# Attention and FFN layer in 32-bit floats: the norm's scaling one tile ahead of its transposition, and the splits of one FFN operand two chunks earlier

## The chip, the cores and the metric

The kernel runs on one core of a Trainium2 chip. The core has a matrix engine (TensorE, PE in the profile), a vector engine (VectorE, DVE), an activation engine (ScalarE, ACT), a general engine (GpSimd, POOL) and a queue engine (SyncE, SP). Each works through its own instructions in order, and they wait for one another by semaphores. Transfers are issued here from SyncE and from POOL. The metric is the device time of one execution in microseconds (us). The profile gives one execution in detail.

## The reference

The input is x, 2 sequences of 2048 tokens, each token a row of 1024 floats. There are two residual sublayers, with a plain layer norm LN ahead of each:

```
y   = x + Attn(LN(x))
out = y + FFN(LN(y))

Attn(z): q, k, v = z Wqkv + bqkv          (256 columns each, one head)
         softmax(q k^T / 16) v Wo + bo
FFN(z):  shared = relu(z up)^2 down        (1024 -> 2048 -> 1024)
         routed = ((z fc1) expert) * r fc2  (latent 512; r: sum of the two largest gate logits)
         LN(shared + routed) * gamma + beta
```

Everything is float32.

## The kernel before

**Precision.** A product of float32 matrices is made of three passes: each operand is split into a high part (rounded by a cast on ScalarE, `xh`, `xha`) and a low part (the rest, by a subtraction on VectorE, `xl`, `xla`), and TensorE sums high x high, low x high and high x low (`Pass3.add`, the matmul is line 130). `split` (lines 142 and 143) issues both parts at once. `split_late` (149 and 150) issues the cast and keeps the subtraction back until the next `flush()`.

**Tiles.** The 4096 tokens are 8 blocks of 512, and each block is 4 tiles of 128 tokens (`NB` = 4). A normalised tile must reach TensorE with the features on the partitions. For that, `transpose_write` transposes 32 x 32 pieces on VectorE (line 213), and a transfer writes the result to a scratch tensor in HBM (`xt_d`, line 218). `fetch_tile` reads it back in another layout (`xt`, line 224), and a split makes the operand of it.

**The q/k/v stage.** Blocks are taken in the order 4 to 7, then 0 to 3; the text counts them in that order from 0 (i = 0 to 7). `qkv_block` makes four tiles of v, then two chunks each of q and k. Its matmuls per block are 96 of 256 columns for v and 96 of 512 columns for q and k. After each piece j it calls `after(j)`, which places work for the next block: after the v tiles, `NormBlock.step(0)` to `step(3)` and then `step(4)` norm, transpose, write and fetch the next block's tiles. After pieces 5, 6 and 7 the first three of them are split. The fourth is split after the first v tile of the next block (`x3`). ScalarE's evictions of q (439) and k (442) stand between these splits.

`NormBlock` has two kinds of statistics. `Moments` makes them on ScalarE (259 to 272, tiles 0 and 2), `Stats` on VectorE (178 to 182, 292, tiles 1 and 3). `normalise` is then the same for both: a reciprocal (276) and a product (282) on VectorE, and the scaling of the row on ScalarE (283).

**What sets the order.** The first seven blocks of this stage, and the whole FFN, stand under `tc.manual_schedule()`: each engine's instructions come in the order in which the code issues them. The last q/k/v block and the attention are ordered by the library's planner. Row buffers are a pool of nine, and large operands are a pool of fourteen. Loads by SyncE for the attention's start (`q_d`, `Wo`) wait for such rows. From i = 4 on, `sum_step` adds 2 MB copies of weights to POOL's queue at the end of a block.

**The FFN.** It takes two blocks (1024 tokens) per pass, b = 0 to 3. Both of its matrix products are made with seven quarter products, named p1 to p7, whose operands are sums and differences of quarters. The loop over `UP` makes the first product in chunks of 12 matmuls: m = 0 to 19 are the interleaved chunks of p1 and p2, m = 20 to 29 are p4, then p6, p5, p3 and p7. The operand of p4 is the split of the second block's tiles (`x_t[1]`, half 1). `X["p4"]` takes its two buffers from the pool, and one tile is split after each of four odd chunks. Each chunk begins with `flush()`. Its result is evicted from the accumulator by ScalarE or VectorE (lines 1000 and 1091 for p2 and p1, 1094 for the latent chunks of p2). Up to chunk 15 the loop also carries the output of the pass before (`out_step`). In pass 0 the second block's norm runs inside these same chunks (`norm2.step`). In later passes it is done in the pass before.

Of the kernel before, what the change touches and what calls it, by code (L numbers as in the profile page):

```python
# [25 lines left out]
def kernel(  # L26
# [33 lines left out]
    NB = W // P  # L60
# [20 lines left out]
    def unit(name, dtype=FR):  # L81
        return up.tile([P, U], dtype, tag="u", name=name)
# [7 lines left out]
    def half(name):  # L90
        return hp.tile([P, W], FP, tag="h", name=name)
# [48 lines left out]
    def split(t, hi, lo, eng=nc.vector):  # L140

        nc.scalar.copy(hi, t)  # L142
        eng.tensor_tensor(lo, t, f32(hi), ALU.subtract)
# [8 lines left out]
    def flush():  # L152
        for f in late_ops:
            f()
        late_ops.clear()
# [55 lines left out]
    def transpose_write(r, q=nc.gpsimd):  # L211
        b = row("xblk")
        nc.vector.transpose(  # L213
            b.rearrange("p (q k i) -> p q k i", q=P // SQ, i=SQ),
            r.rearrange("p (k i q) -> p q k i", k=NCC, i=SQ),
        )
        d = dram.tile([P, C], FP, tag="xt", name="xt_d", bufs=8)
        q.dma_start(out=d, in_=b)
        return d

    def fetch_tile(d, q=nc.gpsimd):

        xt = row("xt")
        q.dma_start(
            out=xt.rearrange("p (a f) -> p a f", a=P // SQ),
            in_=d.rearrange("(a i) (q f) -> (i q) a f", i=SQ, q=P // SQ),
        )
        return xt
# [13 lines left out]
    def split_x(xts, half, t, X, split=split):  # L242
        xv = xts[t].rearrange("p (a k j) -> p k a j", k=NCC, j=SQ)[:, ts(half, NCC // 2)]
        hi, lo = (
            v.rearrange("p (c n) -> p c n", n=W)[:, :, ts(t, P)].rearrange(
                "p c (a j) -> p c a j", j=SQ
            )
            for v in X
        )
        split(xv, hi, lo)  # L250
# [46 lines left out]
    class NormBlock:  # L297
# [5 lines left out]
        def step(self, t):  # L303
            rows, m = self.rows, self.m
            if t == 0:
                m += [Moments(rows[0], "n"), Stats(rows[1])]
                m[0].second()
            if t < NB:
                m[t].normalise()
                if t == 0:  # L310
                    m.append(Moments(rows[2], "n"))
                    m[2].second()
                self.d.append(transpose_write(rows[t]))
                if t == 0:
                    m.append(Stats(rows[3]))
            if t:
                self.x.append(fetch_tile(self.d[t - 1]))
# [19 lines left out]
    def piece(pr, c, n, sl):  # L337
        return tuple(v.rearrange("p (c n) -> p c n", n=n)[:, c, sl] for v in pr)
# [13 lines left out]
    NK = (NIC + NLC) // 2  # L352
# [354 lines left out]
    for n in range(1, NBLK + 1):  # L707
        if n == NBLK:
            X = {p: (unit("xh"), unit("xl")) for p in ("p1", "p2")}
# [117 lines left out]
    def next_piece():  # L827

        while (pieces or staged or cast) and len(ready) < 3:
            if cast:  # L830
                end_piece()
            while pieces and len(staged) < 2:
                stage()
            if staged and not cast:
                cast_piece()
        return ready.pop(0)
# [3 lines left out]
    def acc_bank(name):  # L840
        n_bank[0] += 1
        return bank(psb if n_bank[0] % 3 == 2 else psa, name)
# [153 lines left out]
    def new_x():  # L996
        return unit("xh"), unit("xl")

    def relu(o, v):
        nc.scalar.activation(o, v, AF.Relu)  # L1000

    def square(v):
        nc.scalar.activation(v, v, AF.Square)

    t1 = xts
    with tc.manual_schedule():
        for b in range(NBB):
            if b == 0:
                norm2 = Norm(1)
            x_t = [t1, None]  # L1010
# [3 lines left out]
            def h_at(name, i, n=1):  # L1014

                if i < HU // P:
                    key, q = (name, i // 4), i % 4
                else:
                    key, q = (name in ("11", "12"), "l"), i - HU // P
                    q += 2 * (name in ("12", "21"))  # L1020
                if key not in h:
                    h[key] = unit(f"h{b}", FP)
                return h[key][:, ds((q + 1 - n) * W, n * W)]
# [54 lines left out]
            for m, (p, i) in enumerate(UP):  # L1078
                flush()
                w = next_piece()  # L1080
                if p != "p2":
                    acc[i] = Pass3(acc_bank("pu"), NCC // 2)
                ps = acc[i].ps
                if p == "p2":
                    acc[i].more()
                for c in range(NCC // 2):
                    acc[i].add(piece(w, c, P, slice(0, P)), piece(X[p], c, W, slice(0, W)))
                lat, pair = i >= HU // P, i % 2 and i < HU // P
                c22, c21 = h_at("22", i), h_at("21", i) if m >= 2 * NK else None
                if p == "p1":  # L1090
                    nc.scalar.copy(c22, ps)
                elif p == "p2":
                    if lat:
                        add(h_at("11", i), ps, rwb[0], ALU.mult)
                    else:
                        relu(h_at("11", i), ps)
                        if pair:
                            square(h_at("11", i, 2))
                elif p == "p4":
                    nc.scalar.copy(c21, ps)  # L1100
                elif p == "p6":
                    add(c22, ps, c22, ALU.subtract)
                    add(c21, c21, c22, ALU.subtract)
                elif p == "p5":
                    add(c22, c22, ps, ALU.add)
                elif p == "p3":
                    c12 = h_at("12", i)
                    add(c12, c22, ps, ALU.add)  # L1108
                    if lat:
                        add(c12, c12, rwb[0], ALU.mult)  # L1110
                    elif pair:
                        relu(h_at("12", i, 2), h_at("12", i, 2))
                        square(h_at("12", i, 2))
                else:
                    add(c21, c21, ps, ALU.add)
                    add(c22, c22, ps, ALU.subtract)
                    if lat:
                        add(c21, c21, rwb[1], ALU.mult)
                        add(c22, c22, rwb[1], ALU.mult)
                    elif pair:  # L1120
                        for v in ("21", "22"):
                            relu(h_at(v, i, 2), h_at(v, i, 2))
                            square(h_at(v, i, 2))

                if m % 2 and m < 15:
                    out_step()
                if b == 0 and m in (0, 1, 2, 4, 6, 8, 9, 10, 11, 12, 13):
                    norm2.step()

                if m == 12:  # L1130
                    x_t[1] = norm2.x
                    X["p4"] = new_x()
                if m >= 13 and m % 2 and m < 2 * NK:
                    split_x(x_t[1], 1, (m - 13) // 2, X["p4"], split_late)
                elif m >= 2 * NK and p != "p7":
                    n = {"p4": "p6", "p6": "p5", "p5": "p3", "p3": "p7"}[p]
                    if i == 1:
                        X[n] = new_x()
                    if i % 2 and i < 2 * NB:
                        if p == "p4":  # L1140
                            sums_x(x_t, i // 2)
                        r_, f_ = PLACE[n]
                        split_x(x_t[r_], f_, i // 2, X[n], split_late)

                if m == 0:
                    ga = half("ga")[: 2 * NE, :]
                    nc.scalar.copy(ga, gate_part(X["p1"], 0))
                elif m == 2:
                    gs = half("gs")[: 2 * NE, :]
                    add(gs, ga, gate_part(X["p2"], 1), ALU.add)  # L1150
                    gt = Gate(gs)
                elif (p, i) == ("p4", 1):
                    add(ga, ga, gate_part(X["p4"], 1), ALU.add)
                elif (p, i) == ("p7", 0):
                    add(ga, ga, gate_part(X["p7"], 0), ALU.subtract)
                    gt = Gate(ga)
                if m == 6 or (p, i) == ("p7", 3):
                    gt.largest()
                elif m == 10 or (p, i) == ("p7", 6):
                    rwb[p == "p7"] = gt.spread()  # L1160
                if p == "p7" and i >= NK - 5:
                    step_s()
            X = {}
# [15 lines left out]
            for j, p in enumerate(("p1", "p2", "p6", "p5", "p3", "p7", "p4")):  # L1179
# [12 lines left out]
                for k in range(NK - late):  # L1192
# [4 lines left out]
                    if more:  # L1197
# [3 lines left out]
                        if j >= 5 and k % 2 and k < 2 * NB:  # L1201
                            n = "p1" if j == 5 else "p2"
# [98 lines left out]
```

## Time and profile before

| | us |
|---|---|
| runs | 2402.42, 2394.48, 2394.49 |
| median of the runs | 2394.49 |
| profiled execution | 2396.25 |
| its span | 2394.2 |
| TensorE busy | 2341.5 (98%) |
| VectorE busy | 1461.7 (61%) |
| ScalarE busy | 1133.1 (47%) |
| POOL busy | 297.9 (12%) |
| q/k/v stage, about | 40 to 319 |
| attention, about | 319 to 790 |
| FFN, about | 790 to the end |

The span runs from the first to the last instruction; the execution's own time is 2.05 us longer. A row of a timeline has the start in us, the duration, the engine and line of code, the operation, what it writes and reads, and in brackets how long the engine had been idle before it and what ended that wait. A row of waits has the waiting engine and instruction, what it waited for, the total in us, how many times, and the longest. A row of a table by stretches has the stretch, its length, the busy time of each engine with the number of instructions, the granted share of TensorE's clock, the busy share of the DMA engines and the GB/s.

### The profile page before, as it was taken

Reading aid. Unit: us, or ns where it says so; the run is one execution under the profiler, and the core shown is the slowest. Engines: PE = TensorE matmul, PEld = TensorE weight load, DVE = VectorE, ACT = ScalarE, POOL = GpSimd, SP = SyncE. Lnnn points to the kernel's source line nnn. Section 1 sums busy time; section 2 is a strip of 40 time slices with the busy share of each in tenths; the row PEclk is TensorE's granted clock in tenths of the full one; section 3 lists DMA queues with packets and bytes.
Section 4 is the critical chain, followed back from the end, with each engine's and each line's share of the span. In section 5 each row is a group of like instructions: output and inputs, shape, how many; then the busy total and the mean of one; then the engine's idle time right before and its main releaser. Section 6 shows DMA issues by size and latency. Waiting matters only on the chain.

```text
span 2394.2 us, 29276 instructions
## 1 busy us (share of the span) xinstructions
PE 2341.5 (98%) x10704; PEld 1924.4 (80%) x10704; DVE 1461.7 (61%) x2168; ACT 1133.1 (47%) x1846; POOL 297.9 (12%) x450
## 2 busy tenths in 40 slices
PE   8999899999998999999999999999999999999998
PEld 7888778888886778788777888877888887788886
DVE  5566549888876466797736468644446662435545
ACT  5555445555544553676552274644146354214224
POOL 3322110111110010111210011210000010000001
PEclk9999999999999999999999999999999999999999
DMA  5877883999996666687997779997657799655695
GB/s 187 313 249 270 293 199 101 274 318 318 292 274 180 210 229 192 214 275 255 332 309 234 241 275 333 321 339 249 194 182 268 259 329 296 205 193 185 202 310 191
DMA packets 225807, 603.99 MB, mean 252 GB/s; under 512 B 18768, under 2 KB 80720, under 8 KB 223616
## 3 DMA queue, kind: packets, MB, share of 16 engines
q1 hardware_dynamic: 152160, 334.02, 41.1%
q0 software_dynamic: 73504, 268.11, 36.7%
q8 instruction: 85, 1.39, 0.2%
q14 instruction: 58, 0.48, 0.1%
HBM read 448.96 MB, written 210.76 MB: 276 GB/s over the span
## 4 chain that ended last, share of the span: by engine, by line
PE 78%; issue 9%; DMA 5%; DVE 3%; ACT 3%; POOL 2%; SPq 0%; POOLq 0%; DVEq 0%; ACTq 0%
PE pu L130 30%; PE pd L130 26%; PE ps L130 7%; PE po L130 7%; PE pw L130 3%; PE pg L870 1%; DMA w<-wt 1%; PE pf L130 1%; DMA xt<-xt_d 1%; PE pq L130 1%; DMA w<-w_p 1%; DMA w_p<-w 1%; DVE xblk L213 1%; PE psum L617 1%; ACT xrow L283 1%
## 5 line engine op out<-in xcount | busy, mean ns | idle before, releaser
L130 PE MATMUL pd<-w,sp 128*128 128x512 f32 x3336 | 763.9, 391 | 9.3 <-DVE sp L1055 6.2
L130 PEld LDWEIGHTS pd<-w,sp 128*128 128x128 f32 x3336 | 627.6, 188 | 144.4 <-DVE sp L1055 9.0
L130 PE MATMUL pu<-xh,w 128*128 128x512 f32 x2240 | 694.7, 391 | 7.4 <-ACT w L813 5.9
L130 PEld LDWEIGHTS pu<-xh,w 128*128 128x128 f32 x2240 | 419.6, 188 | 99.0 <-ACT w L813 6.9
L130 PE MATMUL pu<-xl,w 128*128 128x512 f32 x1120 | 436.6, 390 | 2.9 <-DVE xl L150 2.8
L130 PEld LDWEIGHTS pu<-xl,w 128*128 128x128 f32 x1120 | 210.4, 188 | 48.3 <-DVE xl L150 4.6
L1050 ACT CAST sp<-h 128x512 fp32r<-128x512 f32 x238 | 145.7, 618 | 187.9 <-PE pd L130 157.4
L1055 DVE TENSOR_TENSOR sp<-h,sp 128x512 fp32r<-128x512 f32 x238 | 162.4, 688 | 101.0 <-ACT sp L1050 100.7
L813 ACT CAST w<-w 128x512 fp32r<-128x512 f32 x210 | 128.2, 616 | 184.4 <-DMA w<-wt 158.8
L821 DVE TENSOR_TENSOR w<-w 128x512 fp32r<-128x512 f32 x210 | 143.3, 687 | 89.3 <-ACT w L813 84.6
L130 PE MATMUL po<-p,v 128*128 128x512 f32 x768 | 196.4, 393 | 1.4 <-ACT p L142 1.2
L130 PE MATMUL ps<-q,k 128*128 128x512 f32 x768 | 195.9, 393 | 1.9 <-DVE max L560 1.8
L130 PEld LDWEIGHTS ps<-q,k 128*128 128x128 f32 x768 | 142.3, 188 | 36.2 <-DVE max L560 6.9
L130 PEld LDWEIGHTS po<-p,v 128*128 128x128 f32 x768 | 143.5, 189 | 32.2 <-ACT p L142 2.0
L1000 ACT ACTIVATE h<-h 128x1024 f32<-128x1024 f32 x48 | 50.7, 1055 | 208.9 <-DVE h L1108 159.9
L824 POOL DMA_DIRECT2D w_p<-w x140 | 75.5, 539 | 584.3 <-DVE w L821 535.4
L555 ACT COPY s<-ps 128x512 f32<-128x512 f32 x128 | 74.9, 585 | 148.0 <-PE ps L130 147.4
L213 DVE STREAM_TRANSPOSE xblk<-xrow 128x1024 f32<-128x1024 f32 x60 | 120.6, 2010 | 39.0 <-ACT xrow L283 37.7
L150 DVE TENSOR_TENSOR xl<-xt,xh 128x512 fp32r<-128x512 f32 x104 | 71.6, 688 | 119.1 <-ACT xh L149 119.1
L560 DVE TENSOR_TENSOR max<-ps,max 128x512 f32<-128x512 f32 x120 | 82.5, 688 | 44.3 <-ACT s L555 43.9
L130 PE MATMUL pq<-xha,w_h 128*128 128x512 f32 x256 | 99.7, 389 | 0.0
L130 PE MATMUL pq<-xha,w_l 128*128 128x512 f32 x256 | 99.7, 389 | 0.0
(181 smaller groups left out, 3043.1 us busy)
## 6 DMA issues: line engine op xcount, KB each, us to landing
w<-w_p SPq DMA_DIRECT2D x350, 512.0 KB, 3.7
w_p<-w POOLq DMA_DIRECT2D x140, 512.0 KB, 4.6
w<-wt SPq DMA_DIRECT2D x210, 256.0 KB, 3.8
xt_d<-xblk POOLq DMA_DIRECT2D x56, 512.0 KB, 3.5
xt<-xt_d POOLq DMA_DIRECT2D x56, 512.0 KB, 6.4
wt<-in_L_ffn_up_w_dram POOLq DMA_DIRECT2D x9, 2048.0 KB, 26.1
wt<-in_L_ffn_down_w_dram POOLq DMA_DIRECT2D x9, 2048.0 KB, 33.8
xres<-in_L_attn_x_dram SPq DMA_DIRECT2D x32, 512.0 KB, 13.2
```

The costliest lines, as they stand in the source:

```text
L130: nc.tensor.matmul(self.ps, lhsT=a, rhs=b, start=self.i == 0, stop=self.i == self.n - 1, skip_group_check=self.on,)
L150: late_ops.append(lambda: nc.vector.tensor_tensor(lo, t, f32(hi), ALU.subtract))
L213: nc.vector.transpose(b.rearrange("p (q k i) -> p q k i", q=P // SQ, i=SQ), r.rearrange("p (k i q) -> p q k i", k=NCC, i=SQ),)
L283: nc.scalar.activation(self.v, self.v, AF.Identity, scale=rs, bias=nb)
L555: nc.scalar.copy(s["s"][k // 4][:, ts(k % 4, W)], pm)
L560: nc.vector.tensor_tensor(s["max"], pm, s["max"], ALU.max)
L813: nc.scalar.copy(w[:, 0:W], f32(w)[:, W : 2 * W])
L821: nc.vector.tensor_tensor(w[:, W : 2 * W], v[:, W : 2 * W], v[:, 0:W], ALU.subtract)
L824: nc.gpsimd.dma_start(out=kept[key], in_=w.bitcast(FP))
L1000: nc.scalar.activation(o, v, AF.Relu)
L1050: nc.scalar.copy(t[:, 0:W], v)
L1055: add(t[:, W : 2 * W], v, f32(t)[:, 0:W], ALU.subtract)
```

## The change

In `NormBlock.step` the scaling moves one tile ahead. At t = 0 the first tile is normalised, the statistics of tile 2 follow, then tile 1 is normalised, and only then is tile 0 transposed. At t = 1 and 2 the next tile is normalised ahead of the transposition of the present one. At t = 3 there is only the transposition.

In the FFN's first loop the operand of p4 takes its buffers at m = 10 instead of 12 in passes 1 to 3, and its four splits stand after chunks 11, 13, 15 and 17 instead of 13, 15, 17 and 19. Pass 0 keeps 12 and the old places.

```diff
@@ NormBlock.step
             if t == 0:
                 m += [Moments(rows[0], "n"), Stats(rows[1])]
                 m[0].second()
+                m[0].normalise()
+                m.append(Moments(rows[2], "n"))
+                m[2].second()
+
+            if t + 1 < NB:
+                m[t + 1].normalise()
             if t < NB:
-                m[t].normalise()
-                if t == 0:
-                    m.append(Moments(rows[2], "n"))
-                    m[2].second()
                 self.d.append(transpose_write(rows[t]))
                 if t == 0:
                     m.append(Stats(rows[3]))
@@ the FFN's loop over UP
-                if m == 12:
+                m4 = 12 if b == 0 else 10
+                if m == m4:
                     x_t[1] = norm2.x
                     X["p4"] = new_x()
-                if m >= 13 and m % 2 and m < 2 * NK:
-                    split_x(x_t[1], 1, (m - 13) // 2, X["p4"], split_late)
+                if m > m4 and (m - m4) % 2 and (m - m4) // 2 < NB:
+                    split_x(x_t[1], 1, (m - m4) // 2, X["p4"], split_late)
                 elif m >= 2 * NK and p != "p7":
```

## The prediction

> **What bounds the kernel now.** I read the page first, for the engine that sets the end.
>
> ```profile
> span 2394.2 us, 29276 instructions
> ...
> PE 2341.5 (98%) x10704; PEld 1924.4 (80%) x10704; DVE 1461.7 (61%) x2168; ACT 1133.1 (47%) x1846; POOL 297.9 (12%) x450
> ...
> PE 78%; issue 9%; DMA 5%; DVE 3%; ACT 3%; POOL 2%; SPq 0%; POOLq 0%; DVEq 0%; ACTq 0%
> ```
>
> TensorE is busy 98% of the span and carries 78% of the chain that ended last. The built program of the changed kernel has the same TensorE instructions in the same order, so the change can only win or lose time in which TensorE stands still or runs slowly. Next, TensorE's own waits: all of the span's 53 us of idle time is in few places, and three kinds lie where the diff works.
>
> ```profile
> PE pu L130 <- ACT w L813: 5.9, 1, 5.9
> PE pv L130 <- ACT xha L142: 5.9, 1, 5.9
> PE pu L130 <- DVE xl L150: 2.8, 3, 0.9
> PE pv L130 <- DVE xla L143: 1.8, 5, 0.4
> ```
>
> The first row (start of the FFN) is outside the change. The second and fourth are q/k/v blocks that wait for a split tile of the next block; the third is the first chunk of p4 in the FFN passes b = 1, 2, 3. Then the timelines of the seventh block (i = 6), where the long wait arises, one engine after another:
>
> ```profile
> 265.02 1.99 DVE L213 STREAM_TRANSPOSE xblk<-xrow 128x1024 f32<-128x1024 f32 x1 [1.31 <-ACT xrow L283]
> ...
> 269.23 2.03 DVE L213 STREAM_TRANSPOSE xblk<-xrow 128x1024 f32<-128x1024 f32 x1 [1.31 <-ACT xrow L283]
> ...
> 271.55 0.53 POOL L218 DMA_DIRECT2D xt_d<-xblk  x1 [2.93 <-DVE xblk L213]
> ...
> 279.07 0.77 POOL L224 DMA_DIRECT2D xt<-xt_d  x1 [6.22 <-issue]
> ...
> 271.28 0.88 SPq L192 DMA_DIRECT2D xrow<-q_d  x2
> ...
> 285.90 1.14 ACT L142 CAST xha<-xt 128x512 fp32r<-128x512 f32 x2 [12.15 <-DMA xt<-xt_d]
> ...
> 288.19 0.58 PE L130 MATMUL pv<-w_h,xha 128*128 128x256 f32 x1 [5.87 <-ACT xha L142]
> ```
>
> The fourth tile is transposed at 269.23, written at 271.55, fetched back at 279.07 and cast at 285.90. In ScalarE's queue that cast stands ahead of the casts of the third tile, for which TensorE waits from 282.3 to 288.2.
>
> **The change, part 1: the norm.** Nothing is added or removed: per block the same four sets of a reciprocal (0.16), a product (0.16) on VectorE and a scaling (1.24) on ScalarE are issued one tile earlier. No DMA is in the moved step. Now each tile costs VectorE 4.21 us from one transposition to the next (260.82, 265.02, 269.23): 1.99 of transposition, about 0.3 + 0.3 for a v tile's bias and low half, 0.35 for reciprocal and product, and 1.31 of idle time while ScalarE scales. With the scaling a tile ahead, the 1.31 goes three times a block (the first tile keeps it). I walked both queues again with the durations above. Transpositions 2, 3 and 4 start at 259.6, 262.6 and 265.3 instead of 260.82, 265.02 and 269.23, so the last ends 3 x 1.31 = 3.9 us earlier. New waits: VectorE's second reciprocal waits for ScalarE's statistics of tile 2 (done 257.8, used 259.1), and the low half of a v tile waits for its cast, now behind a scaling (done 259.6, used 261.8). Both are met; queued behind them are only transpositions and v tiles, whose accumulators TensorE wants again much later.
>
> What follows in the queues: POOL's tile writes, fetches, row loads, the q write and the 2 MB weight copies all come up to 3.9 us sooner in their old order. In blocks 1 to 5 the q eviction on ScalarE now waits for the last tile write (31.8 us in six waits); freed 3.9 us earlier, it lets the first tile's casts go ahead of TensorE's need. A boundary costs more than its 0.34 us of idle time, since the pipeline restarts: blocks begin 33.94 us apart (a statistics pass at 113.37 and 147.31), and the matmuls need 96 x 0.120 + 96 x 0.228 = 33.4. So 4 x 0.54 = 2.2 us are gained.
>
> The seventh block is the large item. It is tied to TensorE at its start, so I count in its own time. Tile 4 is written at 267.6 instead of 271.55. That write takes 6.98 us from issue to landing, where others take 2.9, because SyncE's two q loads start with it: at 271.28, just as the last transposition ends at 271.26 and frees their row. Those loads therefore move along, and I keep 6.98 and, for the fetch, 6.81. The fetch lands at 282.0 instead of 285.9, the third tile is ready at 284.3, and TensorE stands 2.0 us instead of 5.9. The bounds of this item are no gain (the transfers do not move) and all of it.
>
> All of it is 9.3 us: the two v tiles from 282.16 should take 48 x 0.120 = 5.8 us and end at 297.2. Of that 6.0 is standing, 0.7 the 0.39 wait with its restart, 2.6 half speed (granted clock 0.50 until 294.5). [...] But this trace has waits of 1.81 us (at 1162.75) and 1.84 us (at 1565.21) that are each followed by 3.4 us at 0.50, and one of 1.56 us (at 1181.45) that is not:
>
> ```profile
> 1164.90:1168.30 3.40, 3.40 (x9) 2.64 (x8) 3.37 (x5) 3.37 (x7) 1.01 (x3) 0.50 1.05 377
> 1567.70:1571.00 3.30, 3.30 (x10) 2.57 (x9) 2.98 (x5) 2.28 (x7) 0.00 (x0) 0.50 1.05 303
> 284.30:294.50 10.20, 5.92 (x26) 5.63 (x27) 4.71 (x10) 3.56 (x7) 0.00 (x0) 0.50 0.99 341
> ```
>
> (The seventh column is the granted clock.) I go by the rows: one slow stretch of 3.4 us stays. At 0.213 instead of 0.120 us a matmul it costs 1.5. Left in the block: 2.1 + 0.7 + 1.5 = 4.3, gain 9.3 - 4.3 = 5.0. [...]
>
> **Part 2: p4's splits.** In passes 1 to 3 four casts (0.62, ScalarE) and four subtractions (0.69, VectorE) move two chunks of 2.73 us forward; nothing is added, no DMA, and neither SyncE's nor POOL's queue holds any of it. The low half of the last tile was written behind an eviction that waits for TensorE's own last p2 chunk:
>
> ```profile
> 1258.69 0.69 DVE L1094 TENSOR_TENSOR h<-pu,rwb 128x512 f32<-128x512 f32 x1 [1.43 <-PE pu L130]
> 1259.30 0.68 DVE L150 TENSOR_TENSOR xl<-xt,xh 128x512 fp32r<-128x512 f32 x1
> ...
> 1260.03 0.50 PE L130 MATMUL pu<-xl,w 128*128 128x512 f32 x1 [0.93 <-DVE xl L150]
> ```
>
> That matmul was due at 1258.49 + 2 x 0.23 = 1258.95 and came at 1260.03; with 0.11 of restart behind it, 1.2 us. Two chunks earlier the split is 5 us ahead, so 3 x 1.2 = 3.6 us are gained. What it lands on: chunk 11 on ScalarE, where a square pass ends at 1239.0 and the next eviction waits for TensorE at 1239.65, a hole of 0.67 against 0.62; on VectorE, behind an output tile's scaling that ends at 1239.5 (0.69 more ahead of the last output tile, itself waiting 1.8 for a transfer). The operand's buffers keep their place in the order of allocation. If those covers were gone, an eviction would be 0.6 us later with six accumulators in rotation: nothing for TensorE. Nor is a later stall exposed soon: the next idle time is 300 us on. Bounds: 0 to 3.6; I take 3.6. Pass 0 is untouched.
>
> **Sum.** 2.2 + 5.0 + 3.6 = 10.8 us off a span of 2394.2, so 2383.4; the profiled execution's time is 2396.25, 2.05 above its span, and would be 2385.5. The median of the runs, 2394.49, is 1.8 below that execution: 2394.49 - 10.8 = **2383.7**.
>
> **Rivals.** (A) More is won: the fetch lands in time, because weight copies and row loads ahead of it move up too and the q loads spread out, or no slow stretch follows. [...] For it: a 1.56 us wait left no slow stretch. Against it: the q loads are released by the very transposition that moves.
>
> (B) The seventh block keeps its wait: earlier writes overlap with tile 2's fetch, the write takes longer still, and the fetch lands as before. 2.2 + 3.6 = 5.8: 2388.7. For it: 6.98 and 6.81 us under contention against 2.9 and 4.5 without.
>
> (C) Slower: p4's operand, wanted at chunk 11, gets a buffer that is not free until the last output tile has been written out (issued 1244.11). Then ScalarE holds its cast from 1239.0 to about 1249, evictions queue behind it, and TensorE runs out of its six accumulators. Three passes at 8 us less the 10.8: 2408. It decides from 4 us of standing a pass. Against it: the built order shows no added wait on these casts.
>
> The change doing nothing would leave 2394.5; that needs part 2's subtractions to stay behind the p2 eviction, which the order excludes, so I fold it into B.
>
> **How the numbers follow.** Likeliest, as summed: 0.42, own range 2381.5 to 2387. A 0.38, B 0.12, C 0.08. A measurement of this kernel tells about 0.5% (12.0 us, 2382.5) from no change. A and a little of the likeliest case lie below that: faster 0.41; the rest of the likeliest and B: same 0.51; C: slower 0.08. The range leaves out C and the far end of A: 2376.5 to 2392.
>
> **What would show it.** TensorE's waits: the rows for xl lose three entries of 0.9 and those for xla at least four of 0.34. Transpositions of a block 2.9 us apart, with no idle time for the scaling. The wait for xha near 2.0 us, at 281, with one slow stretch of 3.4 us. I am wrong if the fetch of the fourth tile still takes TensorE past 3 us of waiting, if casts at chunk 11 wait for anything, or if slow stretches appear elsewhere.

## The result, and the profile after

| | before | after |
|---|---|---|
| median of the runs, us | 2394.49 (2393.38 to 2402.42) | 2383.78 (2382.91 to 2387.82) |
| ratio of the times, 95% interval | | 0.9956 (0.9946 to 0.9967) |
| profiled execution, us | 2396.25 | 2384.76 |
| its span, us | 2394.2 | 2382.9 |

The kernel became 10.7 us faster, by the medians of five runs each. Predicted were 2383.7 us and a gain of 10.8. The page after, with the span, the engines, and the chain that ended last:

```profile
span 2382.9 us, 29281 instructions
...
PE 2335.8 (98%) x10704; PEld 1921.8 (81%) x10704; DVE 1461.4 (61%) x2168; ACT 1131.4 (47%) x1846; POOL 298.1 (13%) x450
...
PE 88%; issue 5%; DMA 4%; DVE 1%; ACT 1%; POOL 1%; SPq 0%; POOLq 0%; DVEq 0%; ACTq 0%
```

The number of instructions on each engine listed here is unchanged, and TensorE's matmuls come in the same order, so the 11.3 us of span are time in which TensorE no longer stands or no longer runs slowly. TensorE's waits after:

```profile
PE pd L130 <- DVE sp L1057: 5.6, 7, 1.5
PE pu L130 <- ACT w L815: 5.1, 1, 5.1
...
PE pd L130 <- DMA w<-w_p: 2.0, 1, 2.0
PE pv L130 <- ACT xha L142: 1.9, 1, 1.9
...
PE pu L130 <- ACT xh L149: 1.1, 1, 1.1
...
PE pv L130 <- DVE xla L143: 0.6, 1, 0.6
```

The row for `xl` is gone, with all three waits of 0.9. The row for `xla` has one entry left instead of five, and the wait for `xha` fell from 5.9 to 1.9. A block boundary (the fifth), on ScalarE and then TensorE, before:

```profile
240.58 1.27 ACT L439 ACTIVATE q<-pq,bqk_sb 128x512 f32<-128x512 f32 x2 [5.32 <-DMA xt_d<-xblk]
...
243.13 0.38 PE L130 MATMUL pv<-w_h,xla 128*128 128x256 f32 x1 [0.34 <-DVE xla L143]
```

And after:

```profile
234.98 1.27 ACT L441 ACTIVATE q<-pq,bqk_sb 128x512 f32<-128x512 f32 x2 [7.82 <-DMA xt_d<-xblk]
...
239.75 0.28 PE L130 MATMUL pv<-w_h,xla 128*128 128x256 f32 x1
```

The eviction of q, which stands ahead of the first tile's cast, waits for the block's last tile write in both. That write now lands earlier, and TensorE no longer waits. The timelines of the seventh block after, one engine after another (VectorE, POOL, SyncE, ScalarE, TensorE):

```profile
254.87 2.03 DVE L213 STREAM_TRANSPOSE xblk<-xrow 128x1024 f32<-128x1024 f32 x1
...
257.74 2.03 DVE L213 STREAM_TRANSPOSE xblk<-xrow 128x1024 f32<-128x1024 f32 x1
...
260.32 1.99 DVE L213 STREAM_TRANSPOSE xblk<-xrow 128x1024 f32<-128x1024 f32 x1
...
262.61 0.53 POOL L218 DMA_DIRECT2D xt_d<-xblk  x1 [1.17 <-DVE xblk L213]
...
270.62 0.77 POOL L224 DMA_DIRECT2D xt<-xt_d  x1 [4.87 <-issue]
...
262.34 2.75 SPq L192 DMA_DIRECT2D xrow<-q_d  x2
...
278.46 1.14 ACT L142 CAST xha<-xt 128x512 fp32r<-128x512 f32 x2 [9.04 <-DMA xt<-xt_d]
...
280.75 0.39 PE L130 MATMUL pv<-w_h,xha 128*128 128x256 f32 x1 [1.89 <-ACT xha L142]
281.72 0.39 PE L130 MATMUL pv<-w_h,xla 128*128 128x256 f32 x1 [0.59 <-DVE xla L143]
```

The second to fourth transpositions no longer wait for a scaling; the first of a block still does, for 1.04 us. The first of SyncE's two q loads still starts with the fourth tile's write (262.34 and 262.61), the second comes 2.4 us later, and the fourth tile's cast still stands in front of the third's. The granted clock (the number behind the five engines) behind that wait, and the one short slow stretch that the execution has in the FFN:

```profile
281.00:284.40 3.40, 2.81 (x23) 2.68 (x23) 2.45 (x7) 1.03 (x3) 0.00 (x0) 1.00 1.00 298
284.40:295.00 10.60, 10.60 (x61) 9.29 (x61) 2.04 (x5) 1.50 (x3) 0.00 (x0) 1.00 0.56 199
...
1955.50:1959.30 3.80, 3.80 (x12) 2.95 (x11) 3.75 (x6) 0.24 (x1) 0.56 (x1) 0.55 1.03 285
```

After a wait of 1.89 and one of 0.59 us the clock stayed at 1.00. Last, p4 in pass 1, VectorE and then TensorE:

```profile
1244.43 0.69 DVE L150 TENSOR_TENSOR xl<-xt,xh 128x512 fp32r<-128x512 f32 x1 [2.48 <-ACT xh L149]
...
1248.73 0.69 DVE L1096 TENSOR_TENSOR h<-pu,rwb 128x512 f32<-128x512 f32 x1 [1.43 <-PE pu L130]
...
1248.99 0.39 PE L130 MATMUL pu<-xl,w 128*128 128x512 f32 x1
```

The last subtraction is done 3.6 us before the eviction that it used to follow, and the matmul that waited 0.93 us runs without a wait.

**Where the time went.** Each matmul's start before, minus its start after, shows where the distance grows:

| stretch (time before, us) | gain, us |
|---|---|
| start, up to the first block (loads, not touched) | 0.7 |
| five block boundaries, 107 to 243: 0.27, 0.64, 0.62, 0.63, 0.65 | 2.8 |
| seventh block's tiles, 282 to 297 | 6.3 |
| end of the attention, start of the FFN, pass 0's p4 (752 to 860) | -1.8 |
| p4 in passes 1, 2, 3: 1.23, 1.24, 1.26 | 3.7 |
| slow stretches of the FFN: 1160 to 1183 +1.9, 1558 to 1581 -0.2, 1964 to 1972 -2.1 | -0.4 |
| sum (span 2394.2 to 2382.9: 11.3) | 11.3 |

The last row but one hides two larger terms that happen to cancel: the slow stretches at 1164.9 and 1567.6 are gone, and a new one stands at 1955.9. The 1.8 us given back lie at waits that the change doesn't touch. In pass 0, for example, the cast of p4's last tile stands in ScalarE's queue behind a cast of weights that waits for its transfer; TensorE waited 0.5 us there before and 1.1 after. One execution of each kernel doesn't tell whether they come of the change.

### The profile page after: what moved, and what is told of

Its sections match the earlier page's. It is cut to its first block, busy times and chain, and to the rows that moved or that the text cites. A ratio compares the mean times of both kernels' runs of the same rounds, so it can differ in the third digit from the quotient of the medians.

```text
span 2382.9 us, 29281 instructions
## 1 busy us (share of the span) xinstructions
PE 2335.8 (98%) x10704; PEld 1921.8 (81%) x10704; DVE 1461.4 (61%) x2168; ACT 1131.4 (47%) x1846; POOL 298.1 (13%) x450
## 4 chain that ended last, share of the span: by engine, by line
PE 88%; issue 5%; DMA 4%; DVE 1%; ACT 1%; POOL 1%; SPq 0%; POOLq 0%; DVEq 0%; ACTq 0%
PE pu L130 29%; PE pd L130 26%; PE ps L130 7%; PE pq L130 7%; PE po L130 7%; PE pv L130 4%; PE pw L130 3%; DMA w<-wt 1%; PE pg L872 1%; PE pf L130 1%; DMA xt<-xt_d 1%; DMA w<-w_p 1%; PE psum L619 1%; DMA res<-in_L_ffn_ln_beta_dram 0%; DMA ew<-in_L_ffn_expert_w_dram 0%
```

## The experiments

The theory has four steps. (1) The block boundaries lose a wait of 0.34 us and its restart because the last tile write lands earlier in the new order of the norm. (2) The seventh block's long wait shrinks as far as the fourth tile's fetch lands earlier, because in ScalarE's queue the third tile's casts stand behind it. (3) SyncE's q loads start with the fourth tile's write and stretch it. (4) p4 waits because its last subtraction is queued behind an eviction that waits for TensorE. Rivals: the gain belongs to one part alone; the wait has another cause than the queue's order; the two chunks' distance matters, and not the eviction.

Every time is a median with the ratio to the kernel before on the same chip. The medians of the kernel before were 2396.22 us (the four kernels of the first two headings below), 2394.63 (the held loads, the two on the casts, and the one-chunk splits) and 2394.82 (the rest).

### Each part alone

The norm's new order, with p4 as before:

```diff
+                m[0].normalise()
+                m.append(Moments(rows[2], "n"))
+                m[2].second()
+
+            if t + 1 < NB:
+                m[t + 1].normalise()
             if t < NB:
-                m[t].normalise()
...
```

> Part 1 alone, the splits of p4 at their old place. If the parts are independent, TensorE gains about 0.6 us at each of the first block boundaries (2.9 in all) and 6.3 in the last block, as the changed kernel's matmuls show, and the three waits of 0.93 us for xl in the FFN stay: 2394.5 - 9.2 = about 2385.3. If the parts need each other, or part 2 carries most of the gain, it lies at 2390 or above.

Measured: 2386.85 us, ratio 0.9965 (0.9953 to 0.9978). The new splits of p4, with the norm as before:

```diff
-                if m == 12:
+                m4 = 12 if b == 0 else 10
+                if m == m4:
...
-                if m >= 13 and m % 2 and m < 2 * NK:
-                    split_x(x_t[1], 1, (m - 13) // 2, X["p4"], split_late)
+                if m > m4 and (m - m4) % 2 and (m - m4) // 2 < NB:
+                    split_x(x_t[1], 1, (m - m4) // 2, X["p4"], split_late)
```

> Part 2 alone. Theory: the three waits for xl vanish, 1.2 us each, and the q/k/v stage is as before (one wait of 5.9 us for xha): about 2391. Rival: taking away a 0.9 us wait only moves it to the next thing that is late, and the time stays at 2394.5.

Measured: 2392.4 us, ratio 0.9989 (0.998 to 0.9997). TensorE's waits in the kernel with the norm alone:

```profile
PE pu L130 <- DVE xl L150: 3.7, 4, 0.9
...
PE pv L130 <- ACT xha L142: 1.3, 1, 1.3
...
PE pv L130 <- DVE xla L143: 0.6, 1, 0.6
```

And in the kernel with the splits alone:

```profile
PE pv L130 <- ACT xha L142: 6.5, 1, 6.5
...
PE pv L130 <- DVE xla L143: 1.8, 5, 0.4
...
PE pu L130 <- DVE xl L150: 0.6, 1, 0.6
```

Each part removes its own rows and leaves the other's. What is left of `xl` with the splits alone is pass 0. By the ratios, 0.35% and 0.11% are 8.4 and 2.6 us, together 11.0; both parts at once gave 10.5 (0.44%). The intervals are 4 to 6 us wide (the plain differences of the medians are 9.4, 3.8 and 10.7), and within that the parts add; neither carries the gain alone. By the matmuls' starts the splits alone win 1.23, 1.23 and 1.27 us at the three places, 3.7 in all; that execution lost 5.3 at waits elsewhere, in the attention and the first pass.

### The seventh block alone, and all but the seventh

A second method `step_ahead` holds the new order, and the loop chooses by block:

```diff
+        def step_ahead(self, t):
+            # the new order of step
...
-                norm.step(j)
+                (norm.step_ahead if i == 6 else norm.step)(j)
```

> The scaling goes ahead only in the norm that runs during the seventh block (i = 6), where the long wait arises; the other blocks and the splits are as before. Theory: the last transposition of that block ends 3.9 us earlier and the wait of 5.9 us shrinks to about 2: 5 to 6.3 us off, 2388.2 to 2389.5. Rival: the long wait shrinks because the 2 MB weight copies of the blocks ahead start earlier; then this gains under 2 us and stays above 2392.5.

Measured: 2392.72 us, ratio 0.9988 (0.998 to 0.9996). With `i != 6`:

> The complement: the scaling goes ahead in every block but the seventh. Theory: only the waits of 0.34 us at the block boundaries go, 2.9 us in all, and the wait of 5.9 us stays: about 2391.6. Rival (weight copies): the wait of 5.9 us shrinks here too, and the time is near 2387.

Measured: 2392.72 us, ratio 0.9985 (0.9977 to 0.9994). The boundaries behave as the theory has it: without the seventh block they win 2.8 us by the matmuls' starts, and the long wait stays at 6.3. That also excludes the rival named for both runs, that earlier weight copies shorten it. The seventh block alone did not behave so: it won 2.9 us by the ratio and 2.7 in its execution, where theory and the changed kernel say 5 to 6.3. So I repeated it, and took the sixth and the seventh together (`i in (5, 6)`), to see whether the block ahead must end early for the seventh to gain:

> The run with the scaling ahead in the seventh block alone, a second time beside the one before, for its scatter: 2.9 us off if the first timing stands, 5 or more if that was chance. In its profile the wait for xha shows what the same instructions give in another execution (3.6 us the first time).

> The scaling goes ahead in the norms that run during the sixth and the seventh block (i = 5 and 6), nowhere else; the splits are as before. If the seventh block's gain needs the block ahead of it (its last splits out of the way at the start of the seventh block, its weight copy landed 4 us earlier), this earns 0.6 at one boundary and 5 to 6.3 in the seventh block: 6 us off. If the 2.9 us that the seventh block alone earned is all there is, it earns 3.5.

Measured: 2392.46 us (0.9989, 0.9979 to 0.9999), and 2392.42 us (0.9989, 0.9981 to 0.9997). The repetition confirms a gain of some 2.5 us, and the sixth block added nothing that can be measured. Its boundary shows why, on ScalarE and then TensorE:

```profile
239.22 1.27 ACT L457 ACTIVATE q<-pq,bqk_sb 128x512 f32<-128x512 f32 x2 [9.41 <-DMA xt_d<-xblk]
...
241.78 0.39 PE L130 MATMUL pv<-w_h,xla 128*128 128x256 f32 x1 [0.33 <-DVE xla L143]
```

The block's last tile write took 7.2 us there (5.6 in the changed kernel, 2.9 before), so the eviction of q was not freed sooner, and the wait of 0.33 us stayed. This bears out step 1: what counts is when that write lands. Why it took 7.2 us is open. The waits for `xha` in the three (the seventh, the seventh again, both blocks), each from its own table:

```profile
PE pv L130 <- ACT xha L142: 3.6, 1, 3.6
```
```profile
PE pv L130 <- ACT xha L142: 6.5, 1, 6.5
```
```profile
PE pv L130 <- ACT xha L142: 2.8, 1, 2.8
```

Two things make up the difference between the seventh block alone and in the changed kernel, and the traces show the first. It is in VectorE's queue. In the kernel with the seventh alone, the third split of the block stands ahead of the first v tile's bias, and that runs without any idle time behind it:

```profile
245.77 1.28 DVE L143 TENSOR_TENSOR xla<-xt,xha 128x512 fp32r<-128x512 f32 x2
246.97 0.42 DVE L442 TENSOR_TENSOR v<-pv,bv 128x256 f32<-128x256 f32 x1
```

In the changed kernel the same two are apart, and the bias waits only for its matmuls:

```profile
241.23 1.28 DVE L143 TENSOR_TENSOR xla<-xt,xha 128x512 fp32r<-128x512 f32 x2
242.71 0.42 DVE L426 TENSOR_TENSOR v<-pv,bv 128x256 f32<-128x256 f32 x1 [0.20 <-PE pv L130]
```

Counted from the moment at which TensorE wants the third tile, the bias comes 35.0 us ahead in the one (281.98 - 246.97) and 36.2 in the other (278.86 - 242.71). The seventh block's own norm starts as much later, and the fourth tile's write as well:

| kernel | write issued, us ahead of the need | write, us | fetch, us | landing against the need | wait |
|---|---|---|---|---|---|
| before | 10.8 | 6.98 | 6.81 | +3.6 | 5.9 |
| after | 16.3 | 7.48 | 7.81 | -0.4 | 1.9 |
| norm alone | 16.3 | 7.25 | 7.52 | -1.0 | 1.3 |
| after, splits one chunk earlier (below) | 16.3 | 8.44 | 9.18 | +1.9 | 4.2 |
| seventh alone | 15.2 | 7.65 | 8.29 | +1.3 | 3.6 |
| seventh alone, again | 15.2 | 9.39 | 9.40 | +4.1 | 6.5 |
| sixth and seventh | 15.2 | 7.77 | 7.32 | +0.5 | 2.8 |

The wait is always the landing plus 2.3 us, which is the cast of the fourth tile, a k eviction and the cast of the third (1.14, 0.6 and 1.13 with their overlaps). The 1.1 us of a later start are one part of what the seventh alone lacks. The other thing that moves is the transfers: write and fetch together took 14.8, 15.3 and 17.6 us in the three kernels that have the same instructions in this stage (norm alone, after, one chunk earlier), and 15.9 and 18.8 in the two executions of the seventh alone. So few executions can't say whether they are slower on average where only the seventh block is new. The ratios (8.4 us for all blocks, less 3.6 without the seventh, against 2.6 to 2.9) differ by some 2 us, with intervals about 4 us wide. That rest stays open.

### The order of ScalarE's casts

If the wait comes from the order in the queue, then issuing the fourth tile's split behind the third's ends it, whatever the fetch does. On the changed kernel:

```diff
-        nc.scalar.copy(hi, t)
-        eng.tensor_tensor(lo, t, f32(hi), ALU.subtract)
+        halves[:] = [
+            nc.scalar.copy(hi, t),
+            eng.tensor_tensor(lo, t, f32(hi), ALU.subtract),
+        ]
...
+                third[:] = [list(halves)]
...
-                    x3()
+                    cast, low = third[0]
+                    with tc.issue_after(cast.ins), tc.issue_after(low.ins):
+                        x3()
```

> The changed kernel, and in the eighth block the casts of tile 4 are queued behind those of tile 3 instead of ahead of k's last eviction and tile 3. Theory: what is left of the seventh block's wait (1.89 + 0.59 us in the changed kernel) is only tile 3 standing behind tile 4's fetch in ScalarE's queue; tile 3 landed 6 us before it is wanted and tile 4 is wanted 2.9 us later, so both waits go and 2.5 to 3 us with them: near 2381. Rival: tile 4 is itself late for its own v tile, and the wait moves there at full size: no gain.

Measured: 2380.03 us, ratio 0.9935 (0.9923 to 0.9947). The same edit on the kernel before:

> The same order of casts in the kernel before, with no other change. Theory: tile 3 lands at 280.9 for a wish at 282.2, so of its wait of 6.3 us under 1 is left; tile 4 lands at 285.9 for a wish at 285.1 and costs 2 to 2.5 us with its casts. 3 to 6 us less than before, depending on the slow clock, so about 2390. Rival: the transfers alone set the wait, and the order in the queue is worth under 1 us.

Measured: 2388.49 us, ratio 0.9967 (0.9956 to 0.9979). ScalarE's timeline on the changed kernel with the edit:

```profile
272.52 0.69 ACT L446 ACTIVATE k<-pq,bqk_sb 128x512 fp32r<-128x512 f32 x1 [3.72 <-PE pq L130]
273.11 1.13 ACT L143 CAST xha<-xt 128x512 fp32r<-128x512 f32 x2
277.87 1.14 ACT L143 CAST xha<-xt 128x512 fp32r<-128x512 f32 x2 [3.63 <-DMA xt<-xt_d]
```

And on the kernel before with it:

```profile
279.03 1.14 ACT L143 CAST xha<-xt 128x512 fp32r<-128x512 f32 x2 [3.46 <-DMA xt<-xt_d]
284.66 1.14 ACT L143 CAST xha<-xt 128x512 fp32r<-128x512 f32 x2 [4.49 <-DMA xt<-xt_d]
```

The third tile's cast now comes first, and the fourth's waits for its own transfer with nothing behind it. In the changed kernel no wait is left in those v tiles, though write and fetch took 7.64 and 7.70 us; by the matmuls' starts the block won 9.3 us, 3.0 more than without the edit. On the kernel before, TensorE's wait moved to the fourth tile, where it is 1.9 instead of 5.9 us, and behind it the matmuls start 0.12 us apart, as ahead of it (from 286.28 to 287.00). One line's place in a queue was worth 6.1 us there by the medians and 6.6 by the matmuls' starts in the block, as much as the new order of the norm (6.3). This shows step 2.

### SyncE's q loads behind the last fetch

The two loads move to POOL's queue, behind the fetch of the fourth tile:

```diff
+        fetched[0] = q.dma_start(
-        q.dma_start(
...
-                    start(0, load_row(q_d[0]))
+                    with tc.issue_after(fetched[0].ins):
+                        q0, q1 = (load_row(q_d[a], nc.gpsimd) for a in (0, 1))
+                    start(0, q0)
...
-                    start(1, load_row(q_d[1]))
+                    start(1, q1)
```

> The changed kernel with SyncE's two q loads moved to POOL's queue behind the fetch of tile 4. Theory: they are what stretches tile 4's write (7.5 us against 2.9 elsewhere); without them the write takes 3 to 5 us, the fetch lands 3 to 4 us earlier and the wait for xha is gone: 2.5 to 3 us less than the changed kernel. Rival: the write and the fetch are slow because the tiles' own transfers follow one another more closely; then the write still takes over 6.5 us and the wait stays.

Measured, on the changed kernel: 2379.69 us, ratio 0.9934 (0.9916 to 0.9953). The timelines of POOL and of ScalarE:

```profile
261.56 0.53 POOL L218 DMA_DIRECT2D xt_d<-xblk  x1 [1.16 <-DVE xblk L213]
...
267.16 0.77 POOL L226 DMA_DIRECT2D xt<-xt_d  x1 [2.50 <-issue]
...
269.74 1.07 POOL L192 DMA_DIRECT2D xrow<-q_d  x2
...
275.38 1.14 ACT L142 CAST xha<-xt 128x512 fp32r<-128x512 f32 x2 [6.98 <-DMA xt<-xt_d]
```

With the q loads behind it, the write takes 5.06 us instead of 7.48, and the wait for `xha` is gone; one of 0.6 for `xla` stays. The fetch does not get shorter (8.20): the loads of `Wo`, the q write and the weight copies are issued beside it. So step 3 holds for the write and not for the fetch. The q loads are not the whole of it: the last two kernels below hold them and differ only in the norm, and there the write took 5.69 us in the new order and 2.92 in the old. That fits tile transfers that follow one another more closely in the new order, which was not tested by itself.

### p4's splits one chunk earlier instead of two

```diff
-                m4 = 12 if b == 0 else 10
+                m4 = 12 if b == 0 else 11
```

> The changed kernel with p4's splits after chunks 12, 14, 16 and 18 in passes 1 to 3, one chunk earlier than before instead of two. Theory: the wait came from the last subtraction standing behind the eviction of TensorE's last p2 chunk; one chunk is enough to put it ahead, so no wait for xl of 0.9 us in passes 1 to 3 and the time of the changed kernel. Rival: the split chain is late by more than a chunk; waits of some tenths of a us come back at the three places.

Measured, on the changed kernel: 2382.7 us, ratio 0.9948 (0.9934 to 0.9963). p4 wins 1.23, 1.25 and 1.27 us by the matmuls' starts, as with two chunks, so one chunk is enough. This alone would not tell the eviction from the distance, since a chunk is longer than the wait. The kernel before does: the cast of that tile was done long ahead.

```profile
1254.85 0.62 ACT L149 CAST xh<-xt 128x512 fp32r<-128x512 f32 x1
```

It ended at 1255.47, but the subtraction came only at 1259.30, behind the eviction for which VectorE stood idle until 1258.69. With one chunk it runs at 1250.40 and that eviction at 1252.51: step 4. The q/k/v stage of this kernel is that of the changed kernel, yet its profiled execution waited 4.2 us for `xha`, with a slow stretch of 3.4 behind it (a mean granted clock of 0.87 from 277 to 290), and the seventh block won only 2.6 us there.

### All together, and without the new norm

The cast order and the held loads, both on the changed kernel:

> The changed kernel with both the casts of tile 4 behind those of tile 3 and the two q loads behind the fetch of tile 4. Each alone took the long wait away, so both together have nothing more to win in the seventh block: 2380, like each alone. If the held loads save something elsewhere (shorter transfers at the attention's start), it is below 2378.

Measured: 2377.08 us (2376.9 to 2378.27), ratio 0.9928 (0.9915 to 0.994). Its median is below both, but the intervals of the ratios overlap, and by the matmuls' starts the seventh block won 9.3 us, no more than with the cast order alone, as expected. The 20 us in which the long wait used to fall:

```profile
270.00:290.00 20.00, 20.00 (x135) 18.50 (x135) 7.48 (x15) 4.64 (x10) 3.19 (x6) 1.00 0.97 331
```

TensorE is busy throughout at a granted clock of 1.00; before, the 20 us from 280 had 13.73 us of it at 0.74. Then the same, with the step of the norm put back:

```diff
             if t < NB:
+                m[t].normalise()
+                if t == 0:
+                    m.append(Moments(rows[2], "n"))
+                    m[2].second()
...
-            if t + 1 < NB:
-                m[t + 1].normalise()
```

> The run with both order and held loads, and p4's new splits, but with the norm's scaling in its old place. If the long wait was all that tied the time to the norm, the norm's new order is now worth only the block boundaries, 2.9 us: 2383. If the long wait comes back without the early scaling, it is near 2388.

Measured: 2382.43 us, ratio 0.9947 (0.9934 to 0.996). There is no long wait either, and the five boundary waits are back (1.5 us in five). Its gain of 12.4 us by the medians is the whole of the seventh block's 9.3 and p4's 3.6, as the prediction had sized them (12.9). The new norm adds 5.4 us to that by the medians, of which 2.8 are the boundaries by the traces of the other kernels. The rest I could not place: the profiled execution without it waits 7.3 us instead of 5.1 for `w` at the start of the FFN, and its mean granted clock is 0.995 instead of 0.996; one execution doesn't tell whether that is due to the norm.

## Why the prediction was right, point by point

**The bound.** TensorE's standing and slow time was the right thing to count. The gain lies in the three places named and, for 0.7 us, in the start; 1.8 us were given back elsewhere, and slow stretches of the FFN came and went with a balance of -0.4.

**Boundaries: 2.2 predicted, 2.8 measured.** 0.54 each was near 0.64, and there are five of them: I left out the first, whose wait is shorter and which won 0.27. The experiments with and without the seventh block confirm that they belong to the norm in the other blocks, and q's eviction waits for the tile write as forecast.

**Seventh block: 5.0 predicted, 6.3 measured.** The wait itself was forecast at 2.0 us and came at 1.89, but two steps behind that number were wrong in opposite directions. "The last ends 3 x 1.31 = 3.9 us earlier" was too little: the last transposition starts 8.9 us earlier (269.23 to 260.32), 3.4 of which is TensorE's own shift, so 5.5 in the block's time. Most of the extra 1.6 is the v bias at the block's start, which the late splits no longer hold up (1.1 us, as shown with the seventh alone). And "I keep 6.98 and, for the fetch, 6.81" was too little also: they took 7.48 and 7.81, 1.5 us more together. The landing thus moved by 4.0 us instead of 3.9: two errors that cancelled. In other executions of the same stage these two transfers took up to 8.44 and 9.18, so a forecast of 2.0 was inside a scatter of 1.3 to 4.2. That the q loads move along was right.

**The mis-sized term is the slow stretch.** I kept one of 3.4 us at a cost of 1.5, and none came: 4.0 us of wait and 2.6 of half speed went, less 0.2 that the wait for `xla` grew, which is 6.4. The rows that I went by, 1.81 and 1.84 us followed by half speed, were not a threshold for a wait's length: the 1.89 us here were followed by a granted clock of 1.00, while in the same execution a wait of 1.97 us at 1952.67 is followed by the slow stretch at 1955.9. What decides between such waits is not shown (last section). Three of these four were followed by half speed, so by my estimate a wait forecast at 2.0 us should have been charged three quarters of the 1.5, some 1.1.

**p4: 3.6 predicted, 3.7 measured,** by the mechanism named. The four casts run in the holes of ScalarE as counted, without a wait for a buffer, and pass 0 is as it was.

**The sum.** 10.8 predicted; 11.3 by the spans, 10.7 by the medians. Boundaries (+0.6), the seventh block (+1.3), the start-up (+0.7) and p4 (+0.1) were under-counted by 2.7, and 1.8 and 0.4 were given back where I had assumed that nothing is. The closeness of the total is partly luck of that kind.

**The rivals.** (A) came true in one half, no slow stretch in the block, and not in the other, a fetch in time. The two slow stretches at 1164.9 and 1567.7 vanished as well, but that brought no gain: one of 3.4 us appeared at 1955.9, and the balance is -0.4 us. A slow stretch elsewhere was on my list of signs of being wrong; it came, behind a wait of 1.97 us for a load of weights, and one execution doesn't tell whether the change had a part in it. (A)'s remaining gain was real, as the last experiments show: it took a change in the queues to get it. (B), the wait that stays, is what the execution with the one-chunk splits shows in part (4.2 us); its median is still that of the gain. What it rests on, a write that takes longer in the new order, is there: 5.69 us against 2.92 in the last two kernels. (C) did not happen.

## What to carry to other kernels

Read a long wait through the queue of the engine named in it: where an instruction for a later tile stands first and waits for a transfer, the tile that is wanted now inherits that wait (5.9 us here), and changing the order was worth 6.6 us in the block, as much as hurrying the transfer with the norm (6.3); both gave 9.3. Before moving a step to end a stall, look for the evictions queued in front of it that wait for the stalled engine itself; one place ahead of them was enough here (1.23 to 1.27 us at each of three places). Where a forecast rests on transfers that share the queues, take their scatter (14.8 to 17.6 us here for the two) from several executions before taking one duration to a tenth of a us.

## What was unexpected in the hardware

**The clock after a short wait.** In the profiled executions before and after, half speed (a granted clock of 0.50) followed some waits of TensorE, in stretches of 3.41, 10.24 and 13.65 us. Of its waits of 1.0 us and more, from 40 us on and without those inside a slow stretch, the 13 from 1.00 to 1.68 us were not followed by one, and in the three from 5.13 to 5.94 it began 1.9 to 3.1 us into the wait. In between the length doesn't tell: 1.81 us at 1162.75 and 1.84 at 1565.21 before, and 1.97 at 1952.67 after, were followed by 3.41 us of half speed, which began 0.3, 0.6 and 1.3 us behind the wait's end; 1.89 us at 278.85 after were not. Four waits don't show what decides. By my estimate from them, a wait of 1.8 to 2.0 us costs a slow stretch three times in four.

**Transfers side by side.** The write of the fourth 512 KB tile took 2.92 us with the q loads held and the norm put back, 5.06 and 5.69 with them held in the new order, and 6.98 to 9.39 with the two q loads started beside it. Its fetch took 6.81 to 9.40. Between executions with the same instructions in the stage the sum of the two scattered by 2.9 us, against the 3.9 by which the change was to move the landing.

**Restarts.** A boundary's wait of 0.34 us in the trace cost 0.64 us in the start of all later matmuls, and p4's 0.93 cost 1.23 to 1.27.
